# Two stated times in the planner of a four-layer graph network: layer 1's norm and the LSTM step over row triples

## The chip, the core and the metric

The kernel runs on one core of a Trainium2 chip, in one launch. The metric is device time in microseconds (us), as the median of several executions. The core's engines, as the profile names them: TensorE (PE for matmuls, PEld for weight loads), VectorE (DVE), ScalarE (ACT), GpSimd (POOL) and SyncE (SP, which issues most DMAs here). Everything is computed in float32.

## The reference

The input x is 128 x 64 x 256 (batches, nodes, features), and adj is a 64 x 64 weighted graph. Four layers follow one another, each as x = layernorm(x + layer(x)):

- Layer 0: three times "multiply by a weight, then by adj * adj over the nodes", with relu between.
- Layer 1: U applied around a small network: `h = relu(U.T x W1 + b1)`, `U (h W2 + b2)`, where U holds the eigenvectors of the normalized Laplacian of adj.
- Layer 2: two graph convolutions `relu(adj (x W + b))`, then four LSTMs. For p = 1 to 4 the nodes are cut into windows of p rows, an LSTM runs over the p rows of each window, and its last h replaces the last row of the window. The result of one p is the input of the next:

```
h = relu(einsum('ts,bsh->bth', adj, x @ Wg0 + bg0))
h = relu(einsum('ts,bsh->bth', adj, h @ Wg1 + bg1))
for p in range(1, MAX_SKIP + 1):
    nw = Tv // p
    wins = h[:, :nw * p, :].reshape(Bv * nw, p, Hd)
    last = _lstm_last(Wih[p - 1], Whh[p - 1], bih[p - 1], bhh[p - 1], wins)
    h = h.at[:, idx, :].set(last.reshape(Bv, nw, Hd))
```

- Layer 3: `h = x W + b_lin`, attention among the nodes with scores h h^T masked by the graph, softmax, attention times h, plus b.

## The kernel before, in words

**Tiles.** The 8192 rows of 256 features are 64 tiles of 128 rows (two batches each), and stay in SBUF as X for the whole kernel. Four tiles are a group; there are 16 groups (g = 0 to 15).

**Two phases.** The first phase (until about 876 us) is layer 0 of all groups, with the eigenvectors computed beside it. The second phase runs layers 1, 2 and 3, group by group. The change is in the second phase alone.

**Generators and a planner.** In the second phase each group is a Python generator, `group(g)`, that goes through `layer1`, `layer2` and `layer3`. A generator emits a burst of instructions and then yields a number: the time at which its next burst can begin, as the planner believes. WAYS = 3 groups are in flight. The planner keeps a clock of its own, `now[0]`: every `mm` (L716) adds 2 * max(0.00084 * columns, 0.112) to it, every `turn` (a transpose, L926) 0.11. It takes the first group in the list whose time has come; where none has, it moves its clock to the earliest:

```
        while todo or going:
            while todo and len(going) < WAYS:
                going.append([0.0, 0, todo.pop(0), NT // 4 - len(todo)])
            able = [x for x in going if x[0] <= now[0] + 0.05]
            if not able:
                pick = min(going, key=lambda x: x[0])
                now[0] = pick[0]
            else:
                pick = able[0] if todo else min(able, key=lambda x: x[1] + LEAD * x[3])
```

No code measures anything. The numbers that a generator yields are constants, written at L922 and L923: `MOVE, MIXED, LIN, CONV, NORM, SOFT = 1.2, 1.2, 1.5, 1.8, 5.2, 5.2` and `CELL` by the number of columns of an LSTM step.

**Which orders are fixed by this.** The loop stands in `tc.manual_schedule` for PE: the order of TensorE's instructions is exactly the order in which the bursts are emitted. The order on DVE, ACT and POOL is made by the framework's scheduler from the same emission, with two kinds of copies raised in priority (L953 and L1123). TensorE executes in the order given: where an operand isn't ready, it stands, whatever other group could run.

**The steps of a group**, with the lines that later sections name:

- `layer1`: `mixed` multiplies X by u2 (two PSUM tiles, copied to SBUF by DVE, L953, and by ACT, L954), L965 adds a bias to X, then matmuls by bw1, L971 and L725 (add and relu), matmuls by ut2 and their copy L979 on ACT, matmuls by bw2, L986 (added to X), and the norm of each half of the group.
- A norm (`norm_parts`): for each of two tiles bn_stats and bn_aggr (L551, L552, DVE), then two instructions on POOL (L553, L554: the root), then two DVE instructions that apply it (L564).
- `norm(xs, t, ready, more)` calls it and appends the planner's readiness: `ready.append(now[0] + NORM + more + (0.8 if ready else 0.0))`.
- `layer2`: `mixed` by adT2 (which reads the normed X), cw0, L1067 and a relu (L725), `mixed` by adT2 again, cw1, L1077 and L1079 (relu, written as hT), then five `lstm` calls: p = 1 twice (rows 0 to 31 and 32 to 63), p = 2, 3 and 4. After them hT is copied (L1087, L1088), transposed back (`turn`), added to X (L1096) and normed.
- `lstm(hT, p, first, nw)`: n = 8 * nw columns, 256 for p = 1 and 2, 168 for p = 3, 128 for p = 4. For each of p steps and for each half h of the features: matmuls by wih and, past the first step, by whh, a gate activation each (L1030), the updates of c (L1034, L1036, L1038), tanh of c (L1039), and the new h: L1041 into `hs` for the next step, or, in the last step, L1051 into hT. Then `ready = now[0] + CELL[n]`. In a step past the first, the wih matmuls of its first two units are emitted ahead of `yield ready`; the whh matmuls come after it.
- `layer3`: transposes of X (L1123, L1124 copy them), dw (L1130), transposes back with L1140, the scores (L1146) and the softmax (L1150 to L1168), transposes of the attention (copied at L1166), matmuls by it, L1176 into X, the norm, and a DMA to the output. Groups 14 and 15 are done in two halves.

The yields that depend on the two numbers of the change are the one ahead of the whh matmuls, and the one between the calls of different p, in `lstm` for n = 168; and the two yields in layer 2's first `mixed` (`yield ready[t // 2]`), which hold the adT2 matmuls of a group back until its layer-1 norm is believed done.

Of the kernel before, what the change touches and what calls it, by code (L numbers as in the profile page):

```python
# [590 lines left out]
def rows_norm(tc, pool, x, half, scalar=False):  # L591
    for _ in norm_parts(tc, pool, x, half, scalar):
        pass
# [3 lines left out]
def kernel(  # L597
# [117 lines left out]
    def mm(out, lhsT, rhs, start=True, stop=True):  # L715
        PE.matmul(out, lhsT, rhs, start=start, stop=stop)  # L716
        now[0] += 2 * max(0.00084 * rhs.free_size(), 0.112)
        between()

    def run(out, pairs):  # L720
        for i, (lhsT, rhs) in enumerate(pairs):
            mm(out, lhsT, rhs, i == 0, i == len(pairs) - 1)

    def relu(dst, src):
        S.activation(dst, src, AF.Relu)  # L725
# [194 lines left out]

    now[0] = due[0] = 0.0
    MOVE, MIXED, LIN, CONV, NORM, SOFT = 1.2, 1.2, 1.5, 1.8, 5.2, 5.2  # L922
    CELL = {256: 3.8, 168: 2.2, 128: 1.9}  # L923

    def turn(out, in_):
        PE.transpose(out, in_, ident)  # L926
# [5 lines left out]
    def work2():  # L932
        return tl(pv, [P, 512], "v")
# [3 lines left out]
    def ps4(shape=(P, 512)):  # L937
        return tl(psb, list(shape), "ps")

    def as3(t, a):  # L940
        return t.rearrange("p (a b) -> p a b", a=a)

    def mixed(src, rhs, ready):

        dst = as3(work(), 2)
        ps = [ps4() for _ in range(2)]
        for t in range(4):
            if t % 2 == 0:
                yield ready[t // 2]
            for c in range(2):  # L950
                mm(ps[c][:, t * P:(t + 1) * P], src[:, t, c * P:(c + 1) * P], rhs)
        with tc.high_priority(offset=1500):
            V.tensor_copy(dst[:, 0, :], ps[0])  # L953
        S.copy(dst[:, 1, :], ps[1])  # L954
        yield now[0] + MIXED
        return dst

    def norm(xs, t, ready, more=0.0, scalar=False):
        rows_norm(tc, small, xs[:, t:t + 2, :], half, scalar)
        ready.append(now[0] + NORM + more + (0.8 if ready else 0.0))  # L960

    def layer1(xs, ready):
        a = yield from mixed(xs, u2, ready)
        for t in range(0, 4, 2):
            V.tensor_add(xs[:, t:t + 2, :], xs[:, t:t + 2, :], ub2.unsqueeze(1).to_broadcast([P, 2, D]))  # L965
        h = as3(work2(), 4)
        for t in range(0, 4, 2):
            p = ps4((P, 2, P))
            for j in range(2):
                run(p[:, j, :], [(a[:, k, (t + j) * P:(t + j + 1) * P], bw1[:, k, :]) for k in range(2)])  # L970
            V.tensor_add(h[:, t:t + 2, :], p, wide["b_b1"].unsqueeze(1).to_broadcast([P, 2, P]))  # L971
            relu(h[:, t:t + 2, :], h[:, t:t + 2, :])
            yield now[0]
        yield now[0] + LIN
        z = work2()
        p = ps4((P, 4, P))
        for t in range(4):
            mm(p[:, t, :], h[:, t, :], ut2)
        S.copy(as3(z, 4), p)  # L979
        yield now[0] + MOVE  # L980
        ready = []
        for t in range(0, 4, 2):
            p = ps4((P, 2, D))
            for j in range(2):
                mm(p[:, j, :], z[:, (t + j) * P:(t + j + 1) * P], bw2)
            V.tensor_add(xs[:, t:t + 2, :], p, xs[:, t:t + 2, :])  # L986
            norm(xs, t, ready, 2.0)
            yield now[0]
        return ready

    def lstm(hT, p, first, nw):
# [6 lines left out]
        for t in range(p):  # L998
# [49 lines left out]
            if last:  # L1048

                for h in range(2):  # L1050
# [3 lines left out]
                                           op1=ALU.mult)  # L1054
            ready = now[0] + CELL[n]
            hs = new
# [130 lines left out]
    def group(g):  # L1187
        xs = X[:, 4 * g:4 * g + 4, :]
        ready = [0.0, 0.0]
        ready = yield from layer1(xs, ready)  # L1190
        ready = yield from layer2(xs, g, ready)
        if g in ENDING:

            mine = next(x for x in going if x[3] == g + 1)
            going.append([ready[1], mine[1] + 1, layer3(xs, g, ready, 2, 2), g + 1])
            yield from layer3(xs, g, ready, 0, 2)
        else:
            yield from layer3(xs, g, ready, 0, 4)
# [63 lines left out]
```

## Time and profile before

| what | before |
|---|---|
| median of 6 runs | 2535.6 us (2534.56 to 2539.97) |
| the profiled execution | 2535.18 us |
| its span in the profile | 2533.4 us (1.8 us lie around it) |
| mean granted TensorE clock | 0.996 |
| TensorE busy | 2487.5 us, 98% of the span |
| DVE, ACT, POOL busy | 1407.8, 1090.6, 134.3 us |
| TensorE's busy time in 1515 to 1720 us | 202.64 of 205 us |
| TensorE's busy time in 2337 to 2533.4 us | 179.38 of 196.4 us |

A group line of the page gives, after the line number, engine and operation: the tiles (out<-in), the number of instructions, their busy time and the mean of one in ns, and last the idle time of the engine just before them with the instruction that ended it. A line of the waits view gives "engine, line <- what it waited for", then the sum in us, how often, and the longest. A timeline line gives start, duration of the stretch, engine and instruction, with the number of instructions, and in brackets the idle time ahead of it and what ended that. A matmul in float32 is recorded as two instructions, so a timeline's x8 is four matmuls; a transpose is recorded as one instruction.

### The profile page before, as it was taken

Reading aid. Unit: us, or ns where it says so; the run is one execution under the profiler, and the core shown is the slowest. Engines: PE = TensorE matmul, PEld = TensorE weight load, DVE = VectorE, ACT = ScalarE, POOL = GpSimd, SP = SyncE. Lnnn points to the kernel's source line nnn. Section 1 sums busy time; section 2 is a strip of 40 time slices with the busy share of each in tenths; the row PEclk is TensorE's granted clock in tenths of the full one; section 3 lists DMA queues with packets and bytes.
Section 4 is the critical chain, followed back from the end, with each engine's and each line's share of the span. In section 5 each row is a group of like instructions: output and inputs, shape, how many; then the busy total and the mean of one; then the engine's idle time right before and its main releaser. Section 6 shows DMA issues by size and latency. Waiting matters only on the chain.

```text
span 2533.4 us, 39015 instructions
## 1 busy us (share of the span) xinstructions
PE 2487.5 (98%) x15020; PEld 2190.2 (86%) x15020; DVE 1407.8 (56%) x4996; ACT 1090.6 (43%) x2706; POOL 134.3 (5%) x316
## 2 busy tenths in 40 slices
PE   9999999999999999999999999999999999989997
PEld 7788887888877889998989889898998998978996
DVE  6888777778885433454453543544445445353235
ACT  2344333433333354445444444444544534535454
POOL 0000000000000100000000000000000000010001
PEclk9999999999999999999999999999999999999999
DMA  6000000000000300000000000000000000000000
GB/s 220 1 1 1 1 1 1 1 1 1 1 1 1 117 1 1 10 9 1 9 9 1 9 1 9 9 1 9 1 9 9 1 9 9 1 9 1 1 1 26
DMA packets 24634, 32.09 MB, mean 13 GB/s; under 512 B 2176, under 2 KB 21376, under 8 KB 24448
## 3 DMA queue, kind: packets, MB, share of 16 engines
q1 hardware_dynamic: 24096, 29.32, 3.4%
q8 instruction: 118, 1.93, 0.3%
q14 instruction: 68, 0.56, 0.1%
q10 hardware_dynamic: 352, 0.28, 0.0%
HBM read 21.20 MB, written 8.39 MB: 12 GB/s over the span
## 4 chain that ended last, share of the span: by engine, by line
PE 91%; DVE 5%; POOL 2%; issue 1%; DMA 1%; ACT 0%; SPq 0%; ACTq 0%; POOLq 0%; DVEq 0%
PE ps L716 88%; PE ps L926 2%; POOL ln_rs L554 1%; DVE X L564 1%; DVE ln_st L551 1%; DVE D L51 1%; PE ps L1146 1%; PE pc L93 1%; DMA X<-in_x_dram 1%; POOL ln_rs L553 0%; DVE tw L51 0%; DVE ln_mv L552 0%; DVE X L1176 0%; DVE X L986 0%; DVE X L1096 0%
## 5 line engine op out<-in xcount | busy, mean ns | idle before, releaser
L716 PE MATMUL ps<-w,wih 128*128 128x256 f32 (+2 forms) x4992 | 893.6, 319 | 1.8 <-DVE w L1051 1.8
L716 PEld LDWEIGHTS ps<-w,wih 128*128 128x128 f32 x4992 | 760.4, 191 | 47.8 <-issue 5.7
L1030 ACT ACTIVATE gates<-ps,cbi 128x128 f32<-128x128 f32 (+2 forms) x1248 | 499.4, 410 | 523.0 <-PE ps L716 515.9
L716 PE MATMUL ps<-hs,whh 128*128 128x128 f32 (+2 forms) x3072 | 540.6, 303 | 6.2 <-DVE hs L1041 6.2
L716 PEld LDWEIGHTS ps<-hs,whh 128*128 128x128 f32 x3072 | 453.9, 191 | 32.9 <-issue 11.2
L1036 DVE SCALAR_TENSOR_TENSOR gates<-gates 128x256 f32<-128x256 f32 (+2 forms) x256 | 89.3, 349 | 297.4 <-ACT gates L1030 297.4
L716 PE MATMUL ps<-aw,h 128*128 128x256 f32 x1024 | 227.2, 379 | 0.0
L716 PEld LDWEIGHTS ps<-aw,h 128*128 128x128 f32 x1024 | 192.9, 190 | 25.9 <-ACT h L725 0.5
L725 ACT ACTIVATE h<-h 128x512 f32<-128x512 f32 x128 | 80.6, 629 | 169.5 <-DVE h L51 169.3
L1039 ACT ACTIVATE gates<-c 128x128 f32<-128x128 f32 (+2 forms) x288 | 98.1, 341 | 114.1 <-DVE c L1038 87.9
L1034 DVE SCALAR_TENSOR_TENSOR c<-gates,c 128x128 f32<-128x128 f32 (+2 forms) x192 | 62.5, 326 | 139.4 <-ACT gates L1030 138.1
L1051 DVE SCALAR_TENSOR_TENSOR w<-gates 128x256 f32<-128x256 f32 (+2 forms) x160 | 59.6, 376 | 108.5 <-PE ps L716 73.6
L716 PE MATMUL ps<-ss,tw 128*128 128x256 f32 x512 | 117.9, 380 | 0.0
L716 PE MATMUL ps<-ss,aw 128*128 128x256 f32 x512 | 117.3, 379 | 0.0
L716 PE MATMUL ps<-m,aw 128*128 128x256 f32 x512 | 117.1, 380 | 0.0
L1041 DVE SCALAR_TENSOR_TENSOR hs<-gates 128x128 f32<-128x128 f32 (+2 forms) x192 | 62.7, 327 | 93.6 <-ACT gates L1039 52.4
L716 PE MATMUL ps<-aw,m 128*128 128x512 f32 x256 | 114.5, 593 | 0.0
L553 POOL TENSOR_SCALAR ln_rs<-ln_mv 128x2 f32<-128x2 f32 x96 | 26.2, 273 | 1552.5 <-DVE ln_mv L552 1552.1
L716 PEld LDWEIGHTS ps<-ss,aw 128*128 128x128 f32 x512 | 96.6, 190 | 12.8
L716 PEld LDWEIGHTS ps<-ss,tw 128*128 128x128 f32 x512 | 96.3, 190 | 12.9 <-issue 0.2
L564 DVE TENSOR_SCALAR X<-X,ln_mv,ln_rs 128x256 f32<-128x256 f32 x176 | 64.7, 410 | 75.9 <-POOL ln_rs L554 75.9
L716 PEld LDWEIGHTS ps<-m,aw 128*128 128x128 f32 x512 | 95.6, 190 | 12.6 <-issue 0.5
(294 smaller groups left out, 3094.9 us busy)
## 6 DMA issues: line engine op xcount, KB each, us to landing
X<-in_x_dram SPq DMA_DIRECT2D x30, 256.0 KB, 6.0
out_dram<-X SPq DMA_DIRECT2D x28, 256.0 KB, 2.1
wih<-in_c_ih_dram SPq DMA_DIRECT2D x4, 1024.0 KB, 7.3
aw<-in_a_w_dram SPq DMA_DIRECT2D x3, 1024.0 KB, 10.4
whh<-in_c_hh_dram SPq DMA_DIRECT2D x3, 1024.0 KB, 9.4
out_dram<-X SPq DMA_DIRECT2D x8, 128.0 KB, 1.7
aw<-in_a_w_dram SPq DMA_DIRECT2D x1, 512.0 KB, 6.0
cw<-in_c_w_dram SPq DMA_DIRECT2D x2, 256.0 KB, 5.1
```

What stands on the lines that cost most here:

```text
L51: return getattr(self.engine, name)(out, *args, **kw)
L553: nc.gpsimd.tensor_scalar(rs, mv[:, :, 1], EPS, None, op0=ALU.add)
L564: nc.vector.tensor_scalar(x[:, t, :], x[:, t, :], mv[:, t, 0:1], rs[:, t:t + 1], op0=ALU.subtract, op1=ALU.mult)
L716: PE.matmul(out, lhsT, rhs, start=start, stop=stop)
L725: S.activation(dst, src, AF.Relu)
L926: PE.transpose(out, in_, ident)
L1030: S.activation(gate[q][:, h, :], pp, AF.Tanh, bias=bias[:, j:j + 1], scale=0.5 if q == "g" else 0.25)
L1034: V.scalar_tensor_tensor(c[:, h, :], gate["f"][:, h, :], 1.0, c[:, h, :], op0=ALU.add, op1=ALU.mult)
L1036: V.scalar_tensor_tensor(to, gate["i"][:, h, :], 1.0, gate["g"][:, h, :], op0=ALU.add, op1=ALU.mult)
L1039: S.activation(gate["i"][:, h, :], c[:, h, :] if p > 1 else to, AF.Tanh, scale=0.5)
L1041: V.scalar_tensor_tensor(new[:, h, :], gate["o"][:, h, :], 1.0, gate["i"][:, h, :], op0=ALU.add, op1=ALU.mult)
L1051: V.scalar_tensor_tensor(hT[:, h, slice(first + p - 1, first + nw * p, p), :], gate["o"][:, h, :].rearrange("p (w b) -> p w b", b=8), 1.0, ...
```

## The change

Two constants of the planner are made larger: the time from the last matmul of an LSTM step with 168 columns (p = 3) to its h, from 2.2 to 3.4, and the extra time stated for layer 1's norm, from 2.0 to 3.3. Both are used only as yields. No instruction is added or removed; the order of TensorE's instructions, and with it the emission order that the other engines' orders are made from, can change wherever the planner compares these times with its clock.

```diff
--- before.py
+++ after.py
@@ -920,7 +920,7 @@
 
     now[0] = due[0] = 0.0
     MOVE, MIXED, LIN, CONV, NORM, SOFT = 1.2, 1.2, 1.5, 1.8, 5.2, 5.2
-    CELL = {256: 3.8, 168: 2.2, 128: 1.9}
+    CELL = {256: 3.8, 168: 3.4, 128: 1.9}
 
     def turn(out, in_):
         PE.transpose(out, in_, ident)
@@ -984,7 +984,7 @@
             for j in range(2):
                 mm(p[:, j, :], z[:, (t + j) * P:(t + j + 1) * P], bw2)
             V.tensor_add(xs[:, t:t + 2, :], p, xs[:, t:t + 2, :])
-            norm(xs, t, ready, 2.0)
+            norm(xs, t, ready, 3.3)
             yield now[0]
         return ready
 
```

## The prediction

> **What bounds the kernel now.** I read the page first: busy time by engine, then the chain that ended last, then the groups.
>
> ```profile
> PE 2487.5 (98%) x15020; PEld 2190.2 (86%) x15020; DVE 1407.8 (56%) x4996; ACT 1090.6 (43%) x2706; POOL 134.3 (5%) x316
> PE 91%; DVE 5%; POOL 2%; issue 1%; DMA 1%; ACT 0%; SPq 0%; ACTq 0%; POOLq 0%; DVEq 0%
> L716 PE MATMUL ps<-w,wih 128*128 128x256 f32 (+2 forms) x4992 | 893.6, 319 | 1.8 <-DVE w L1051 1.8
> L716 PE MATMUL ps<-hs,whh 128*128 128x128 f32 (+2 forms) x3072 | 540.6, 303 | 6.2 <-DVE hs L1041 6.2
> ```
>
> TensorE holds 98% of the span and 91% of the chain. The change adds and removes no matmul, so only TensorE's idle time can move. The waits view splits that idle time:
>
> ```profile
> PE ps L716 <- DVE X L564: 6.9, 5, 2.8
> PE ps L716 <- DVE hs L1041: 6.2, 5, 1.3
> PE ps L716 <- ACT v L725: 5.4, 3, 3.9
> PE ps L716 <- DVE w L1051: 1.8, 2, 1.5
> PE ps L716 <- ACT v L979: 0.7, 1, 0.7
> ```
>
> [...] The first two rows are the two waits whose stated times are lengthened: layer 1's norm handed to layer 2 (L564), and h of an LSTM step (L1041). Four of the five of each stand together, 205.5 us apart, once for every two groups. The timeline of one such place:
>
> ```profile
> 1435.33 0.73 DVE L564 TENSOR_SCALAR X<-X,ln_mv,ln_rs 128x256 f32<-128x256 f32 x2 [0.57 <-POOL ln_rs L554]
> 1435.89 1.13 PE L716 MATMUL ps<-adT,X 128*128 128x128 f32 x8 [1.02 <-DVE X L564]
> ...
> 1436.88 0.80 POOL L553 TENSOR_SCALAR ln_rs<-ln_mv 128x2 f32<-128x2 f32 x1 [1.59 <-DVE ln_mv L552]
> ...
> 1438.51 0.73 DVE L564 TENSOR_SCALAR X<-X,ln_mv,ln_rs 128x256 f32<-128x256 f32 x2 [0.90 <-POOL ln_rs L554]
> 1439.16 0.33 DVE L1041 SCALAR_TENSOR_TENSOR hs<-gates 128x168 f32<-128x168 f32 x1
> 1439.54 1.12 PE L716 MATMUL ps<-hs,whh 128*128 128x168 f32 x6 [1.34 <-DVE hs L1041]
> ```
>
> TensorE stands 1.02 us for a norm, then 1.34 us for an h whose L1041 lies in DVE's queue behind that norm's second half. One place before that matters, because after the change its order is met again and again. TensorE first, DVE second:
>
> ```profile
> 1189.34 1.04 PE L926 MATMUL ps<-ident,w 128*128 128x128 f32 x8
> 1190.21 1.89 PE L716 MATMUL ps<-w,wih 128*128 128x256 f32 x8
> 1191.94 1.05 PE L716 MATMUL ps<-ut,v 128*128 128x128 f32 x8
> 1193.67 1.13 PE L716 MATMUL ps<-bw,v 128*128 128x256 f32 x4 [0.68 <-ACT v L979]
> ...
> 1196.75 2.42 PE L716 MATMUL ps<-w,wih 128*128 128x256 f32 x10 [1.51 <-DVE w L1051]
> ```
>
> ```profile
> 1189.98 1.29 DVE L1096 SCALAR_TENSOR_TENSOR X<-ps,X 128x512 f32<-128x512 f32 x2 [1.11 <-PE ps L926]
> ...
> 1193.53 0.73 DVE L564 TENSOR_SCALAR X<-X,ln_mv,ln_rs 128x256 f32<-128x256 f32 x2 [0.81 <-POOL ln_rs L554]
> ...
> 1195.62 0.73 DVE L564 TENSOR_SCALAR X<-X,ln_mv,ln_rs 128x256 f32<-128x256 f32 x2 [0.90 <-POOL ln_rs L554]
> 1196.28 0.75 DVE L1051 SCALAR_TENSOR_TENSOR w<-gates 128x256 f32<-128x256 f32 x2
> ```
>
> The hT write (L1051) of one group waits in DVE's queue behind the whole norm of another group, with two POOL round trips inside it. From the first transpose (1189.34) to the wih matmul behind L1051 (1196.75) is 7.41 us.
>
> **What the skill says.** The Trainium skill, "PSUM — Partial Sum Buffer", section "Engine vs sequencer instructions": VectorE's, ScalarE's and GpSimdE's queues are strict FIFO, and matmuls run in program order. The trace agrees: L1041 at 1439.16 and L1051 at 1196.28 start only as the norm ahead of them ends. "SBUF — State Buffer", section "Who interferes with whom": a DVE instruction with two SBUF inputs contends with a GpSimd instruction that reads SBUF. The trace agrees: L553 takes 0.80 us at 1436.88, beside an L965 addition of two SBUF tiles, and 0.22 us at 1434.29 beside none. "Perfetto Trace Analysis", section "DVE / Act Engine Instruction (TENSOR_ADD, Activation, etc)": a profiled end is the write's acknowledgement, and the semaphore travels after it. Here that costs 0.05 us (L1041 ends 1439.49, TensorE starts 1439.54).
>
> **The change, part by part.** I took the order of the changed kernel's built program (no times), gave each matmul the pitch that this trace shows from start to start (128x256 0.432 us, 128x168 0.285, 128x128 0.224, a transpose 0.109), and so got TensorE's distance from each producer's cause to its consumer. Where that distance is shorter than the hand-over measured in this trace, there is a wait. An idle of the page costs 0.165 us more than it shows, since back-to-back matmuls overlap by that much (four of 1.03 us start every 0.865).
>
> *What goes.* The two numbers only change the readiness that the planner believes: +1.2 us on p=3 steps, +1.3 us on layer 1's norm. In the changed order the adT2 matmuls come 8.6 us or more after the norm's cause (now 7.22 against a need of 8.09 at the four bad places), and the second whh2 pair 4.0 us after its own where it came 3.2 us after. Both targeted waits vanish from the repeating part. Since all later bursts move, the other idles of this stretch go too: 0.68, 1.51 and 0.28 (1193 to 1229), four times 1.02 + 1.34 = 9.44, and 2.77 + 3.90 (2257 and 2262). Sum 18.6 in 13 idles, plus 13 x 0.165 = 2.1: **20.7 us**. The first part, up to 876 us, has the same order in both. The tail from 2463 has it too: its 9.4 us of idle stay.
>
> *What comes, repeating.* The changed order settles into a period of one group, about 101.3 us of TensorE work, six times. In each it has: transposes, two wih0 units, ut2, bw2, wih1. That is the order at 1189 with the room shorter. TensorE's own work from the first transpose to wih1 is 8 x 0.109 + 4 x 0.432 + 4 x 0.224 + 4 x 0.432 = 5.23 us. DVE's order in that stretch is the one in the fence, so the hand-over is 7.41. The loss is 2.18 us per period: 0.84 already at bw2, which directly follows ut2 and needs its copy L979 (0.68 + 0.165), the rest at wih1. Six periods: **13.1 us**. What is behind the stalled matmul is all of TensorE's queue, so nothing covers it.
> Bounds of this cost: 0.84 if L1051 doesn't end up late, 3.4 if both POOL trips in it (1.13 and 1.20 us) are stretched as at 1436.88, where one took 1.72. I take 2.18, the measured case of the same order.
>
> *Two smaller ones, repeating.* cw0 needs its DVE copy L953. From the last layer-3 burst (w,v at 1218.90) to that copy I follow 1227.33 for the L1038 ahead of it plus 0.68 for the copy: the matmul is due 8.76 us after, and needs 9.09: 0.33, five times, **1.7 us**. The p=4 call's first step now stands directly behind another group's cw1, so two hT activations (L1079, 1.15 us each) are ahead of its gates in ACT's queue: from the end of cw1 its second h takes 4.35 us, and TensorE wants it (whh3) at 3.80 to 3.90. Some 0.5 us, six times: **3.0 us**.
>
> *One-offs on the way to the new period* (places between 999 and 1611 us): adT2,w 0.1, whh2 1.9 (DVE's order of 1435 once more: 16.4 us needed from its cause, 14.5 there), cw0 0.6 and 0.9, whh2 0.4 and 0.5, transposes of X 2.3 and of w 0.6, dw 0.1: **7.4 us**. At 2212 to 2290, where 2.77 + 3.90 stood, I find no wait, but slacks of 0 to 0.5 us.
>
> *Nothing.* ACT and DVE do the same instructions, at 43% and 56% busy. Output DMAs move with their groups; their 2.1 us ends in DRAM, and no instruction waits for it but the last. SP's queue holds nothing else. Each group has its own rows of X, so no transfer frees a buffer that another waits for.
>
> *Sum.* 13.1 + 1.7 + 3.0 + 7.4 = 25.2 against 20.7: **+4.5 us**. The profiled execution took 2535.18 (span 2533.4 and 1.8 around it), so 2539.7; the median of the runs is 0.4 above that execution, so 2540.1.
>
> **Rivals.** 0.2% is 5.1 us, about what a measurement of this kernel can tell from no change: slower is above 2540.7, faster below 2530.5.
>
> *Stretched chain (slower still).* The POOL trips in the repeating place meet a DVE instruction with two SBUF inputs, or the late wih1 makes the dw matmul behind it late (margin 0.35 to 0.75 us). For it: the 1.72 us trip. Against it: at 1193 the same DVE order gave 1.13 and 1.20. Two trips x 0.59 x 6 = +7.1: 2547.2.
>
> *The hT write is not late (not slower).* In the repeating place only the ut2 to bw2 hand-over is paid, 0.84. This is decided by the chain from the first transpose to L1051: at 6.07 us or less (5.23 + 0.84) it hides, and it measures 7.41. It would take DVE doing L1051 ahead of the norm's second half, so that a POOL trip and two L564 (1.20 + 0.73) drop out. Against it: the built order has L1051 behind them. Then 6 x 1.34 = 8.0 less: 2532.1.
>
> *The waits vanish and nothing comes instead (faster).* 2535.6 - 20.7 = 2514.9. Against it: bw2 stands directly behind ut2 in the new order, and that hand-over is measured.
>
> *The change does not do what it says.* Stated times might not move a burst. Excluded: TensorE's order differs from 880 us on.
>
> **How the numbers follow.** My sum 0.60; stretched chain 0.20; hT write not late 0.15; nothing instead 0.05. The sum's own spread is 2535 to 2546: 0.45 to 0.55 on whh3, the one-offs (half to double of 7.4, since margins under 0.3 us are left out), and the smaller slacks. Of its 0.60, 0.33 lies above 2540.7, as waits that I have missed only add, and 0.27 within. Slower: 0.33 + 0.20 = 0.53. Same: 0.27, and 0.07 of the third case: 0.34. Faster: 0.08 + 0.05 = 0.13. The range takes the whole sum, the nearer half of the stretched case and most of the third: 2530 to 2550. Likeliest case alone: 2535 to 2546.
>
> **What would show it.** Right: the waits view has L564 to adT2 and L1041 to whh2 nearly gone, and "w L1051" near 6 x 1.2 = 7 us and "v L979" near 4 us in their place; a period near 101.3 + 2.2 + 0.3 + 0.5 = 104.3 us. Wrong: no L1051 wait (third case), an L1051 wait above 2 us each or a dw wait in each period (stretched), or a targeted wait that stays.

## The result and the profile after

| what | before | after |
|---|---|---|
| median | 2536.8 us (38 runs) | 2543.3 us (18 runs) |
| ratio, 95% interval | | 1.0025 [1.0019, 1.0032] |
| span of the profiled execution | 2533.4 us | 2541.7 us |

The changed kernel is slower by 6.5 us, or 0.25%. The forecast was 2540.1, slower by 4.5 (the median of before, then from six runs, was 2535.6). In the later runs of the kernel before, executions at a granted clock of 0.995 or 0.996 took 2534.4 to 2537.7 us and those at 0.993 took 2539.1 to 2541.8, so a median depends on how many there are of each. The page of the kernel after, in the lines that were shown of before (busy time, chain, two groups):

```profile
PE 2493.5 (98%) x15020; PEld 2190.1 (86%) x15020; DVE 1407.6 (55%) x4996; ACT 1092.8 (43%) x2706; POOL 132.8 (5%) x316
...
PE 88%; DVE 7%; POOL 2%; ACT 1%; issue 1%; DMA 0%; SPq 0%; ACTq 0%; POOLq 0%; DVEq 0%
...
L716 PE MATMUL ps<-w,wih 128*128 128x256 f32 (+2 forms) x4992 | 892.5, 319 | 6.5 <-DVE w L1051 6.5
...
L716 PE MATMUL ps<-hs,whh 128*128 128x128 f32 (+2 forms) x3072 | 540.2, 303 | 5.3 <-DVE hs L1041 5.3
```

No instruction has become dearer; the chain passes through TensorE a little less (88% for 91%) and through DVE more (7% for 5%). The idle time in front of the wih matmuls has grown from 1.8 to 6.5 us. The waits view of the kernel after:

```profile
PE ps L716 <- DVE w L1051: 6.5, 6, 1.1
PE ps L716 <- DVE hs L1041: 5.3, 10, 1.7
PE ps L716 <- ACT v L979: 4.0, 6, 0.7
PE ps L716 <- DVE w L953: 3.7, 7, 2.1
...
PE ps L716 <- ACT w L725: 2.5, 2, 2.1
PE ps L716 <- ACT v L725: 1.5, 2, 1.2
PE ps L926 <- DVE X L564: 1.5, 1, 1.5
```

The row "L716 <- DVE X L564" (6.9 us before, in front of the adT2 matmuls) is gone, and so is the repeated wait for h of the p=3 step. In their place stand two rows of six waits each: L1051, the hT write, at 1.1 us, and L979, the copy of the ut2 product, at 0.7 us. One of the six places, TensorE first and DVE second:

```profile
1707.31 1.04 PE L926 MATMUL ps<-ident,w 128*128 128x128 f32 x8
1708.18 1.89 PE L716 MATMUL ps<-w,wih 128*128 128x256 f32 x8
1709.91 1.05 PE L716 MATMUL ps<-ut,v 128*128 128x128 f32 x8
1711.64 1.99 PE L716 MATMUL ps<-bw,v 128*128 128x256 f32 x8 [0.68 <-ACT v L979]
1714.72 1.56 PE L716 MATMUL ps<-w,wih 128*128 128x256 f32 x6 [1.08 <-DVE w L1051]
```

```profile
1707.95 1.29 DVE L1096 SCALAR_TENSOR_TENSOR X<-ps,X 128x512 f32<-128x512 f32 x2 [1.11 <-PE ps L926]
...
1711.49 0.73 DVE L564 TENSOR_SCALAR X<-X,ln_mv,ln_rs 128x256 f32<-128x256 f32 x2 [0.82 <-POOL ln_rs L554]
...
1712.31 0.39 DVE L1036 SCALAR_TENSOR_TENSOR gates<-gates 128x256 f32<-128x256 f32 x1
1713.60 0.73 DVE L564 TENSOR_SCALAR X<-X,ln_mv,ln_rs 128x256 f32<-128x256 f32 x2 [0.90 <-POOL ln_rs L554]
1714.25 0.75 DVE L1051 SCALAR_TENSOR_TENSOR w<-gates 128x256 f32<-128x256 f32 x2
```

It is the place at 1189 us of the kernel before, now once in each period of 104.6 us (1711.64, 1816.25 and so on): from the first transpose to the wih matmul 1714.72 - 1707.31 = 7.41 us, to the hundredth what it was there.

**Where the time went.** I compared each matmul's start with its neighbour's, against the usual pitch of the same pair, from 900 to 2455 us of both profiles. Idle time costs 20.7 us before (13 waits) and 26.5 after (31 waits): +5.8. The first matmul after a wait takes 0.32 us to its successor where 0.216 is usual, 0.1 us more: with 18 more waits, +1.7. And some matmuls of the kernel before run at half rate after its long waits at 2257 and 2262, which the kernel after doesn't have: -1.4. With 0.2 of small differences the sum is +6.3. The two spans differ by 8.3: the other 2.0 us lie in the tail, where the same matmuls took the last 73.4 us of the span before at a mean granted clock of 0.92, and the last 75.3 us after at 0.88. That the medians differ by 6.5, so close to 6.3, is in part chance, since they mix executions at different clocks.

### The profile page after: what moved, and what is told of

It is laid out like the page before. It is cut to its first block, busy times and chain, and to the rows that moved or that the text cites. A ratio compares the mean times of both kernels' runs of the same rounds, so it can differ in the third digit from the quotient of the medians.

```text
span 2541.7 us, 38996 instructions
## 1 busy us (share of the span) xinstructions
PE 2493.5 (98%) x15020; PEld 2190.1 (86%) x15020; DVE 1407.6 (55%) x4996; ACT 1092.8 (43%) x2706; POOL 132.8 (5%) x316
## 4 chain that ended last, share of the span: by engine, by line
PE 88%; DVE 7%; POOL 2%; ACT 1%; issue 1%; DMA 0%; SPq 0%; ACTq 0%; POOLq 0%; DVEq 0%
PE ps L716 85%; PE ps L926 2%; POOL ln_rs L554 1%; DVE X L564 1%; DVE ln_st L551 1%; DVE D L51 1%; PE ps L1146 1%; PE pc L93 1%; POOL ln_rs L553 1%; DVE X L1096 0%; DVE ln_mv L552 0%; DVE tw L51 0%; DVE X L1176 0%; ACT gates L1030 0%; ACT w L1079 0%
## 5 line engine op out<-in xcount | busy, mean ns | idle before, releaser
L716 PE MATMUL ps<-w,wih 128*128 128x256 f32 (+2 forms) x4992 | 892.5, 319 | 6.5 <-DVE w L1051 6.5
L716 PEld LDWEIGHTS ps<-w,wih 128*128 128x128 f32 x4992 | 760.8, 191 | 55.5 <-DVE w L1051 8.9
L716 PE MATMUL ps<-hs,whh 128*128 128x128 f32 (+2 forms) x3072 | 540.2, 303 | 5.3 <-DVE hs L1041 5.3
L716 PEld LDWEIGHTS ps<-hs,whh 128*128 128x128 f32 x3072 | 454.4, 191 | 29.6 <-issue 8.1
L1036 DVE SCALAR_TENSOR_TENSOR gates<-gates 128x128 f32<-128x128 f32 (+2 forms) x256 | 89.1, 348 | 262.6 <-ACT gates L1030 262.6
L716 PE MATMUL ps<-aw,h 128*128 128x256 f32 x1024 | 227.2, 379 | 0.0
L716 PEld LDWEIGHTS ps<-aw,h 128*128 128x128 f32 x1024 | 192.9, 190 | 25.9 <-ACT h L725 0.5
L716 PE MATMUL ps<-ss,tw 128*128 128x256 f32 x512 | 117.9, 380 | 0.0
L716 PE MATMUL ps<-ss,aw 128*128 128x256 f32 x512 | 117.3, 379 | 0.0
L716 PE MATMUL ps<-m,aw 128*128 128x256 f32 x512 | 117.1, 380 | 0.0
L716 PE MATMUL ps<-aw,m 128*128 128x512 f32 x256 | 115.5, 597 | 0.0
L1051 DVE SCALAR_TENSOR_TENSOR w<-gates 128x256 f32<-128x256 f32 (+2 forms) x160 | 59.5, 376 | 94.6 <-PE ps L716 65.9
L716 PEld LDWEIGHTS ps<-ss,aw 128*128 128x128 f32 x512 | 96.6, 190 | 12.8
L716 PEld LDWEIGHTS ps<-ss,tw 128*128 128x128 f32 x512 | 96.3, 190 | 12.9 <-issue 0.2
L716 PEld LDWEIGHTS ps<-m,aw 128*128 128x128 f32 x512 | 95.6, 190 | 12.6 <-issue 0.5
L553 POOL TENSOR_SCALAR ln_rs<-ln_mv 128x2 f32<-128x2 f32 x96 | 24.7, 258 | 1562.3 <-DVE ln_mv L552 1561.8
L564 DVE TENSOR_SCALAR X<-X,ln_mv,ln_rs 128x256 f32<-128x256 f32 x176 | 65.1, 409 | 74.3 <-POOL ln_rs L554 74.2
```

The source lines that it names most:

```text
L553: nc.gpsimd.tensor_scalar(rs, mv[:, :, 1], EPS, None, op0=ALU.add)
L564: nc.vector.tensor_scalar(x[:, t, :], x[:, t, :], mv[:, t, 0:1], rs[:, t:t + 1], op0=ALU.subtract, op1=ALU.mult)
L1036: V.scalar_tensor_tensor(to, gate["i"][:, h, :], 1.0, gate["g"][:, h, :], op0=ALU.add, op1=ALU.mult)
L1051: V.scalar_tensor_tensor(hT[:, h, slice(first + p - 1, first + nw * p, p), :], gate["o"][:, h, :].rearrange("p (w b) -> p w b", b=8), 1.0, ...
```

## Experiments

The theory: the two numbers do nothing but choose one of many orders; the loss of this order is that the hT write stands in DVE's queue behind another group's norm, once per period. (The digits are those of the code: wih1 are the input weights of the LSTM with p = 2, whh2 and whh3 the recurrent weights with p = 3 and 4, cw0 those of the first graph convolution.) Times are compared with the runs of the kernel before on the same chip.

**One number alone, twice.** The diff of the first is `CELL[168]` 2.2 to 3.4; of the second, the norm's 2.0 to 3.3.

> Only the p=3 step's stated time is lengthened (2.2 to 3.4); the norm's stays at 2.0. If the loss came from this number alone and the two numbers' effects simply added, this kernel would lie between before and after, at +0 to +6.5 us. My theory is that a number acts only through the order that it happens to bring, so that halves don't add up: laying the built order of each engine out with the durations of the two profiles gives about +17 us here, to some 2554.

> Only the stated time of layer 1's norm is lengthened (2.0 to 3.3); the p=3 step's stays at 2.2. If effects added, this and the kernel with the other number alone would sum to the +6.5 us of the change. My theory expects no such sum: the built order laid out with the profiles' durations gives about +2 us, some 2538.8, with most of the two targeted waits replaced by others.

Measured: the p=3 number alone 2552.65 against 2537.54 (ratio 1.0051 [1.0039, 1.0064]), +15.1 us; the norm's number alone 2544.79 against the same, 1.0024 [1.0018, 1.0031], +7.3. The effects don't add: 15.1 + 7.3 is over three times the change. The waits view of the kernel with the p=3 number alone:

```profile
PE ps L716 <- DVE w L1051: 12.5, 11, 1.6
PE ps L716 <- ACT v L979: 6.8, 10, 0.7
```

It is the same repeating place, met ten times instead of six: this number brings the period, and it begins four groups sooner. My +2 for the norm's number was wrong. That kernel has 13 idle places in the same stretch, as before; they cost only 2 us more. What I had left out stands in its timeline and, behind it, in the windows view (length, busy time of each engine with the number of instructions, granted clock, DMA share, GB/s):

```profile
1645.73 1.22 PE L716 MATMUL ps<-hs,whh 128*128 128x168 f32 x6 [2.24 <-DVE hs L1041]
1646.74 1.33 PE L716 MATMUL ps<-w,wih 128*128 128x168 f32 x4
1647.86 1.33 PE L716 MATMUL ps<-hs,whh 128*128 128x168 f32 x4
1648.98 1.26 PE L716 MATMUL ps<-w,wih 128*128 128x168 f32 x4
1650.07 0.73 PE L716 MATMUL ps<-hs,whh 128*128 128x168 f32 x4
```

```profile
1645.00:1650.00 5.00, 4.27 (x18) 4.27 (x19) 2.61 (x8) 1.71 (x5) 0.00 (x0) 0.66 0.01 3
```

Four matmul instructions of 168 columns take 1.33 us where 0.73 is usual, for some 4 us after an idle time of 2.24 us; the granted clock of these 5 us is 0.66. By the comparison of starts, matmuls that are slower than usual away from any wait cost this kernel 7.3 us, and the one before 3.0: +4.3, together with +2.0 of idle time most of the 7.3. (Of the 7.3, 5.9 lie in stretches of lowered clock, of the 3.0 some 1.5.)

**DVE's order.** TensorE's and GpSimd's orders are the changed kernel's, instruction by instruction. DVE's differs at 336 of 4996 places and ACT's at 28 of 2706.

```diff
-                    V.scalar_tensor_tensor(to, gate["i"][:, h, :], 1.0, gate["g"][:, h, :], op0=ALU.add, op1=ALU.mult)
+                    with tc.high_priority(offset=40): V.scalar_tensor_tensor(to, gate["i"][:, h, :], 1.0, gate["g"][:, h, :], op0=ALU.add, op1=ALU.mult)
...
             if last:
+              with tc.high_priority(offset=40):
                 for h in range(2):
```

> The changed kernel with TensorE's order untouched, but with the two DVE instructions behind an LSTM step's gates (L1036 and the hT write L1051) raised in priority, so that they stand ahead of another group's norm in DVE's queue. My theory (the repeating loss at wih1 is the hT write queued behind the norm): the 1.08 us L1051 wait goes in all six periods, 6 x 1.25 = 7.5 us, less about 1 for norms that come later: some 6 us faster than the changed kernel, about 2537; the 0.68 us L979 wait stays. Rival (three groups are in short steps at once, so the next operand is late whatever DVE does first): no gain, 2543; some other producer has the wait.

Measured: 2534.99 against 2537.54, 0.9986 [0.9979, 0.9993]: 2.6 us faster than before, so 9.1 faster than the changed kernel (8.3 between the two medians themselves). From start to start of the same matmuls, those that the changed kernel runs from 1606 to 2244 us, its six periods, take 631.0 us instead of 637.3, and those from 1000 to 1300 us 2.8 us less. The same place, TensorE and DVE:

```profile
1704.58 1.04 PE L926 MATMUL ps<-ident,w 128*128 128x128 f32 x8
...
1708.91 1.99 PE L716 MATMUL ps<-bw,v 128*128 128x256 f32 x8 [0.68 <-ACT v L979]
1710.74 2.75 PE L716 MATMUL ps<-w,wih 128*128 128x256 f32 x12
```

```profile
1707.08 0.41 DVE L1036 SCALAR_TENSOR_TENSOR gates<-gates 128x256 f32<-128x256 f32 x1
1707.41 0.42 DVE L1051 SCALAR_TENSOR_TENSOR w<-gates 128x256 f32<-128x256 f32 x1
...
1708.21 0.41 DVE L1051 SCALAR_TENSOR_TENSOR w<-gates 128x256 f32<-128x256 f32 x1
1709.21 0.74 DVE L564 TENSOR_SCALAR X<-X,ln_mv,ln_rs 128x256 f32<-128x256 f32 x2 [0.59 <-POOL ln_rs L554]
```

The hT write is done at 1708.6, ahead of the norm's first L564, and wih follows bw2 without a gap. L979's 0.68 stays, as expected. What is late next shows too: the copy L953 for cw0 now costs 0.92 us per period instead of 0.33, since a raised L1051 and a norm's L564 stand ahead of it. The rival (the next operand is late anyhow) is wrong for the largest part. What this kernel doesn't separate is L1036 from L1051: in the changed kernel both lie behind a piece of the norm (1712.31 and 1714.25), and both were raised.

**The copy alone.** Again TensorE's order is the changed kernel's.

```diff
-        p = ps4((P, 4, P))
         for t in range(4):
-            mm(p[:, t, :], h[:, t, :], ut2)
-        S.copy(as3(z, 4), p)
+            p = ps4((P, 2, P)) if t % 2 == 0 else p
+            mm(p[:, t % 2, :], h[:, t, :], ut2)
+            if t % 2: S.copy(as3(z, 4)[:, t - 1:t + 1, :], p)
```

> The changed kernel with TensorE's order untouched, but the ut2 product goes to two PSUM tiles with an ACT copy (L979) for each half, so that the first half is ready by the time that bw2 needs it. My theory: the wait at bw2 (0.84 us of loss) and the one at wih1 are one 2.09 us loss, whose end is set by the hT write; the first goes and the second grows to take its place, so the gain is about 1 us or less (2542.5), and the L1051 wait is near 1.8 to 1.9 us each. Rival (the losses are separate and add): 6 x 0.84 = 5 us faster, 2538, with the L1051 wait still at 1.08.

Measured: 2542.73 against 2537.54, 1.0016 [1.0009, 1.0023]: +5.2, so 1.4 us better than the change's +6.5 (0.6 between the two medians themselves; the intervals overlap), not 5. Its timeline:

```profile
1706.07 1.04 PE L926 MATMUL ps<-ident,w 128*128 128x128 f32 x8
...
1709.74 1.99 PE L716 MATMUL ps<-bw,v 128*128 128x256 f32 x8
1713.48 2.86 PE L716 MATMUL ps<-w,wih 128*128 128x256 f32 x12 [1.75 <-DVE w L1051]
```

The wait at bw2 has gone, and the one at wih1 has grown from 1.08 to 1.75. From the transposes to wih1 it is 1713.48 - 1706.07 = 7.41 us once more. The two waits are one loss, whose end the hT write sets. In the six periods nothing at all is gained: the same matmuls take 637.4 us, and 637.3 with one copy. The gain lies in the first group's start, where the wait of cw0 at 885 us falls from 2.1 to 1.1 us.

**Both.** The two edits together.

> The changed kernel with both edits of the two kernels before it: the DVE instructions behind an LSTM step's gates raised in priority, and the ut2 product in two PSUM tiles with a copy each. With two copies alone the gain was 0.6 us, as the hT write then set the end. My theory: with that write out of the way the wait at bw2 counts for itself, so the same edit is worth several times as much here: up to 6 x (0.84 + 0.1) = 5.6 us against the kernel with the priority alone (2535.0), less what the cw0 wait takes of it; some 3 to 4, about 2531.5. Rival (two copies are worth about half a us wherever they stand): 2534.4.

Measured: 2529.67 against 2537.05, 0.9969 [0.9956, 0.9981]: -7.4, where the priority alone gave -2.6. The copies are worth 4.8 us here and 1.4 there. Not all of it is the wait at bw2: in the six periods the same matmuls take 628.3 us instead of 631.0, so 2.7 us here and nothing there. Most of the rest lies again in the first group's start, where the cw0 wait is halved and a lowered clock that the profile with the priority alone has (from 885.7 us) doesn't come. An edit that hides a wait is worth nothing while a later wait of the same chain stands, and something once that one has gone: 2.7 of 6 x 0.84 = 5.0 us, as bw2 still waits 0.24 us for its copy in each period.

**The priority without the change.** The times before, with the priority edit.

> The kernel before, with its own stated times, and only the priority of the two DVE instructions (L1036, L1051) raised. If the queueing behind norms is a matter of the new order alone, nothing is gained but the 1.5 and 0.3 us L1051 waits (2535). My theory: the waits of the order before, too, stand behind norms in DVE's queue; the built order laid out with the profiles' durations gives about 8 us less, 2529.5. Stated times before and priority together then beat stated times after and priority (2535.0) by some 5 us, so that the change is a loss in both.

Measured: 2527.03 against 2537.05, 0.9961 [0.9947, 0.9974]: -10.0. Idle time costs 11.6 us instead of 20.7. The two waits that the change was aimed at:

```profile
PE ps L716 <- DVE X L564: 6.2, 5, 4.0
...
PE ps L716 <- DVE hs L1041: 0.8, 1, 0.8
```

The waits for h at 1439 us and its likes have gone: what the longer time of the p=3 step was to cover is made by DVE's order. The norm's waits are shorter (four of 0.55 us instead of 1.02) but not gone, and the last has grown from 2.8 to 4.0 us. The numbers that the change lengthened are worse than the old ones with the priority too (2535.0 against 2527.0; by the differences from before, 7.4 us).

**A shorter number.** `CELL[168]` 2.2 to 1.8, nothing else.

> The kernel before with the p=3 step's stated time made shorter, 1.8, where the change makes it longer (3.4); nothing else. If the number's direction matters (too short a stated time brings bursts that stand), this is slower than before. My theory, by which a number only picks one of many orders: some 7 us faster, 2530.

Measured: 2540.05 against 2537.05, 1.0005 [0.9997, 1.0013]: not to be told from no change, and the 7 us gain that I expected isn't there. The profile shows the idle time that I counted on (16.3 us for 20.7), but matmuls slower than usual away from any wait cost 7.4 us in it for 3.0, and 11 more waits cost some 1.1 in first matmuls. The single times lie between 2534.4 and 2541.5 and go with the granted clock: six at 0.996 or 0.997 take at most 2537.6 us, seven at 0.993 or 0.994 at least 2540.0. Why the clock differs from one execution to the next is not shown.

**Other times.** The priority edit, with the norm's number 2.4 instead of 2.0 and `CELL[128]` 2.3 instead of 1.9.

> Other stated times, with the same priority: p=3 step 2.2 as before, layer 1's norm 2.4, p=4 step (128 columns) 2.3 where it was 1.9. Found by laying out the built orders of some 150 sets of constants with the durations of the two profiles: idle time of the repeating part nearly gone, 18 us less than before, 2518 to 2520. If stated times closer to the true ones were what helps, the p=3 step at 2.2 (its true need is up to 5.8 where it queues behind a norm) would make this one worse than the changed kernel with priority, 2535.0.

Measured: 2510.89 against 2537.05, 0.9895 [0.9881, 0.9908]: -26 us, faster than any kernel above. The windows view of the same stretch, of before, of after and of this kernel in this order:

```profile
900.00:2455.00 1555.00, 1536.41 (x10236) 1406.15 (x10235) 681.22 (x1926) 718.67 (x1793) 77.03 (x156) 1.00 0.02 5
```

```profile
900.00:2455.00 1555.00, 1533.59 (x10179) 1398.76 (x10178) 678.25 (x1916) 717.84 (x1783) 75.56 (x156) 1.00 0.02 5
```

```profile
900.00:2455.00 1555.00, 1554.45 (x10438) 1426.38 (x10437) 692.36 (x1960) 728.36 (x1820) 79.72 (x160) 1.00 0.02 5
```

TensorE is busy for 1554.45 of 1555 us: one wait of 0.55 us is left. Which of the two numbers does it is not separated. In the same stretch it does 10438 matmul instructions where the changed kernel does 10179. Three more kernels say what makes this so. The same times without the priority:

> The stated times of the fastest kernel so far (norm 2.4, p=3 step 2.2, p=4 step 2.3), without the priority of the two DVE instructions. Priority alone was worth 10 us on the times before. If the two gains are separate, this is 26 - 10 = 16 us faster than before, 2521. My theory: the times were picked for the hand-overs that the priority makes short; without it the same bursts find h and hT queued behind norms again, and laying out the built orders gives some 6 us faster than before, 2530, with L1051 or L1041 waits in the waits view.

Measured: 2532.12 against 2536.73, 0.9979 [0.9971, 0.9987]: -4.6, not -16. Its waits view has one large row, h behind a norm, six times:

```profile
PE ps L716 <- DVE hs L1041: 13.4, 6, 2.2
```

The change's two numbers put into it:

> The fastest kernel so far with the two numbers of the change put into it (p=3 step 3.4, norm 3.3). If the change's two numbers did harm only through the hT write in DVE's queue, they cost nothing here (2511). My theory: they bring the order in which bw2 directly follows ut2 in each period, with cw0 and whh3 close behind their producers, whatever DVE does first; the built order gives some 18 us more than the fastest, 2527 to 2534.

Measured: 2530.34 against 2536.73, 0.9974 [0.9964, 0.9985]: 19.8 us of the gain of 26 are gone, and the waits at bw2, cw0 and whh3 are back in each period:

```profile
PE ps L716 <- DVE w L953: 5.9, 6, 2.1
PE ps L716 <- ACT v L979: 4.1, 6, 0.7
...
PE ps L716 <- DVE hs L1041: 2.4, 7, 0.6
```

Its six periods take 631.0 us, as those of the changed kernel with the priority do. So the hT write behind the norm is the largest loss of the change's order, and not the only one: with it out of the way, the other hand-overs of that order still lose.

And the two copies added to it:

> The fastest kernel so far with the ut2 product in two PSUM tiles and two copies. There is no wait at bw2 in its repeating part, so the copies hide nothing there: about 1 us faster at most, by the first group's start (the cw wait at 885 us fell from 2.1 to 1.05 us when this was done to the changed kernel), 2510. If two copies were an advantage in themselves, it would be 3 to 5 us, as on the changed kernel with the priority.

Measured: 2509.22 against 2536.73, 0.9889 [0.9876, 0.9903], 1.4 us better than without by the differences from before, within their intervals. There is nothing at bw2 to hide.

## Why the prediction was right, step by step

- **What goes, 20.7 us.** Right: all 13 idles of before have left their places, and by starts they cost 20.71. Left out: what a wait costs beyond its idle time. After the 3.90 us at 2262 the kernel before ran at half rate for some 3 us, which is 1.4 us more that the change takes away. One reading was off: 7.22 us against a need of 8.09 at the four bad places would be a loss of 0.87 us, where the trace has 1.02 + 0.165 = 1.19. The 8.6 us of the changed order are enough for either.
- **What comes, repeating, 13.1 us.** Measured 6 x 2.09 = 12.5, with the split as forecast (0.84 at bw2, 1.25 at wih1). The 7.41 us hand-over was met exactly. The DVE-order run shows that what stands ahead of the hT write and of its L1036 in DVE's queue is the cause, and the two-copies run that the write's end sets the whole loss.
- **The smaller repeating ones.** cw0 1.7: measured 5 x 0.33 = 1.6. whh3 3.0: measured 6 x 0.45 = 2.7.
- **One-offs, 7.4 us.** Measured 9.6, in eight places. The difference is one place: the adT2 matmuls at 1019 us, put at 0.1, lost 2.26. The errors of the others cancel by luck (the transposes of X 1.6 for 2.3, and up to 0.3 more at some of the rest). I had taken the hand-over of places where DVE's queue was free. Here L1067 stood behind a norm and two hT writes (L1051 at 1017.02 and 1017.65, L1067 at 1017.99). It is the mechanism that I had named for wih1, not looked for at a second place.
- **The tail and the first part unchanged.** Right but for the lower clock in the tail of this one execution (2.0 us).
- **The sum, +4.5.** Idle time +5.8; the missing term is 0.1 us per wait for its first matmul (18 more waits, +1.7), and the half rate of before takes 1.4 back. The loss per wait should have been 0.27 us over the idle time shown, not 0.165. The direction was a narrow call: the likeliest time, 2540.1, lay 0.6 us under the prediction's own border to slower, which had 0.53 of the chance.
- **The rivals.** POOL trips were not stretched. The hT write was late. That nothing comes instead, and that the stated times do not move a burst, are both refuted by the waits view.
- **The GpSimd trip beside DVE.** The L553 of 0.22 us at 1434.29 was not beside none: an L1036 with two SBUF inputs (1434.12, 0.30 us) was in its last 0.13 us. The comparison stands all the same: the L553 at 1040.49, beside no DVE instruction at all, took 0.22 us, and the six beside an L965 took 0.56 to 0.80.

## What to carry to other kernels

Where an order is planned from stated times, a changed time in one place can be a new order everywhere: judge it by the order's own hand-overs, not by the wait that it was to remove. Before giving a wait more time, look at what its producer is queued behind: here two raised instructions on DVE were worth 10 us. Other times, chosen with them in place, brought 26 us together with them and 4.6 us without. Of two waits in one chain, only the later one's removal counts until it has gone.

## What was not expected of the hardware

- Each wait costs more than its idle time: the first matmul of 256 columns behind one takes 0.320 us to its successor, where 0.216 is usual.
- An idle time of 2.24 us can be followed by half rate for 3 to 4 us. It was at two of four such places in the norm-only kernel (waits that end at 1645 and 2058 us, not at 1440 and 1852), and at three of six in the times-alone kernel, every second one in both. The windows view of the norm-only kernel, in windows of 3.41 us (the second number is TensorE's busy time, the 0.50 or 1.00 near the end the granted clock), shows what tells them apart:

```profile
1438.41:1441.82 3.41, 1.64 (x11) 1.64 (x12) 2.25 (x6) 0.72 (x3) 0.70 (x1) 1.00 0.00 0
1643.21:1646.62 3.41, 1.17 (x8) 0.92 (x8) 2.51 (x7) 0.34 (x1) 1.37 (x2) 1.00 0.00 0
1646.63:1650.04 3.41, 3.41 (x14) 3.41 (x13) 0.99 (x4) 1.71 (x5) 0.00 (x0) 0.50 0.02 5
1851.43:1854.84 3.41, 1.88 (x13) 1.88 (x14) 2.47 (x7) 0.97 (x4) 0.46 (x1) 1.00 0.00 0
2056.23:2059.64 3.41, 1.17 (x9) 1.13 (x9) 2.51 (x7) 0.33 (x2) 1.13 (x2) 1.00 0.00 0
```

The starts of lowered clock in one profile lie whole multiples of 3.413 us apart (1646.63 and 2059.64 are 121 of them), so these windows can be laid on that grid. In all thirteen profiles, from 880 to 2455 us, the clock is lowered 15 times: each time right behind a window of the grid in which TensorE was busy for at most 0.42 of the time, and never behind one with 0.45 or more. The busy shares above are 0.48, 0.34, 0.55 and 0.34 at the four waits, and 0.45, 0.34, 0.53, 0.34, 0.60 and 0.38 in the times-alone kernel, where the second, fourth and sixth were followed by half rate. So the length of a wait doesn't decide alone; it counts how much of it falls into one window. The Trainium skill, "TensorE: Matmul & The Clock Gate", section "What's actually happening", gives a half-rate state after an idle window of about 3.4 us. The traces agree on the half rate and on the length, but the window need not be idle: 0.42 busy was still followed by it. Two lines of the kernel before, at its longest wait, show half rate as well: eight instructions take 2.08 us, where the same eight of 128 columns took 1.05 at 1191.94:

```profile
2262.10 2.08 PE L716 MATMUL ps<-ut,v 128*128 128x128 f32 x8 [3.90 <-ACT v L725]
2263.97 1.56 PE L716 MATMUL ps<-adT,X 128*128 128x128 f32 x8
```
